# Paying out the convolution more densely beside two passes of matmuls, a new order of the second pass's first steps, and weights that load into space that is free earlier

## The chip, the cores and the metric

The kernel runs on one core of one Trainium2 chip. The metric is the device time in microseconds (us) from launch to end, as the median of several executions. Before the change it is 3131.01 us (three runs, 3129.59 to 3134.88). All data is float32.

The core has a matrix engine (PE, with a separate row PEld for its weight loads), a vector engine (DVE), a scalar engine (ACT), a GpSimd engine (POOL), and a queue (SP) that issues the transfers between DRAM, where all large tensors live, and the on-chip memory.

## What is computed

Two layers on an image batch of shape (2, 56, 56, 384). Layer 0 is neighbourhood attention (12 heads, 7 x 7 windows) followed by an MLP; layer 1 is a depthwise 3 x 3 convolution with four exponential scans, between two projections, followed by an MLP:

```python
# layer 0
h = neighborhood_attention(layer_norm(x), w_qkv, rpb, w_proj)
x = x + h
x = x + gelu(layer_norm(x) @ w1 + b1) @ w2 + b2              # 384 -> 1536 -> 384
# layer 1
p = layer_norm(x) @ w_in + b_in                              # 384 -> 768
local = depthwise_conv_3x3(p)                                # 768 channels
mixed = 0.25 * (scan_right(local) + scan_left(local)         # y[t] = 0.6 y[t-1] + 0.4 x[t]
                + scan_down(local) + scan_up(local)) + local
x = x + layer_norm(mixed) @ w_out + b_out                    # 768 -> 384
x = x + gelu(layer_norm(x) @ w1 + b1) @ w2 + b2
```

So three stages follow one another: attention; a *first pass* over tokens (MLP of layer 0, then the projection w_in of layer 1); and a *second pass* (projection w_out and MLP of layer 1). Between the two passes stands the convolution with its scans, which DVE computes channel block by channel block (6 blocks of 128 channels per image) while PE runs the passes.

## The kernel before

The passes run over groups of 512 tokens (4 tiles of 128). Group 0 of the first pass has only one tile. The order of instructions in the two passes is the order of the program text, on every engine. The convolution is cut into small steps, and a bookkeeper, `Beside`, hands them out between the matmuls:

```python
class Beside:
    def __init__(self):
        self.jobs, self.due, self.finished, self.idle = [], 0.0, set(), True
        self.late, self.rate = [], 0.85
    # ...
    def go(self, worth):                 # called after every few matmuls
        self.due += self.rate * worth    # pays out steps until the debt is gone
        while self.due > 0.0:
            step = self.step()           # emits one step, returns its size in us
            if step is None: self.due = 0.0
            else:            self.due -= step

    def until(self, name):               # emits steps until that job is done
        while name not in self.finished: self.step()
        # ...
MLP, PRO, ROW = 2.0, 2.5, 5.6            # first pass: per hidden block, per w_in block, per tile
MLP_D, OUT_D, ROW_D = 1.85, 2.2, 6.3     # second pass
```

A job is a `Band` (rows lo to hi of one channel block: one ACT copy, eight multiply-adds on DVE for the taps, two scans along the rows, one mixing operation) or, when all bands of an image are in, a `Columns` job (the scans along the columns: it loads the result of the bands back from DRAM, ACT turns it, DVE scans it and adds it to `mix_d`). Job `(1, 5)` is the last one: image 1, block 5.

```python
class Columns:
    def turn(self):                      # 4 ACT copies out of the loaded halves
        # ...
        nc.scalar.copy(t[...], self.loc[h][:, :, at].rearrange("p h w -> p w h"))
    def steps(self):
        if not self.lines:
            self.turn()
            yield 2.5
        # ... scans on DVE, then mixed += share * scanned, then the store
```

The pools for the passes are opened when attention's pools are closed, so they share its space. The loads of the first pass:

```python
wp = ctx.enter_context(tc.tile_pool(name="w", bufs=1))        # w1, w2, w_in, w_out ...
gp = ...; io = ...                                            # hidden blocks; x, xn, hT, xc, mx
# ...
xs = {0: load_group(x1f, groups[0], "xa")}
w1, w2, s2 = load_w(0)                                        # w1 in three pieces
nc.sync.dma_start(out=w_in, ...)
load_w2(w2, s2)                                               # w2 in three pieces
xs[1] = load_group(x1f, groups[1], "xa")
load_row(0, "b2_0"); load_row(1, "b_out")
nc.sync.dma_start(out=w_out, ...)
```

First pass, one group (`hidden` is three matmuls and a Gelu on ACT; `tokens` is twelve or six matmuls into one of two banks, which DVE empties):

```python
for g, (t0, n) in enumerate(groups):
    for m in range(NHID):                                     # 12
        hid.append(hidden(w1, m, hT, n, "L0_conv_b1"))
        if m == 3 and g < last: norm_next = norm_of(x_next)   # DVE statistics, close on POOL
        if m == 2 and waiting is not None: waiting = normalize_x2(*waiting)
        if m == 6 and g < last: xn_next = normalized(norm_next, x_next, n_next)   # ACT
        beside.go(MLP)
    if waiting is not None: project_in(*waiting)              # 6 blocks of w_in, beside.go(PRO)
    if g < last: hT = channels(xn_next, ...)                  # PE transposes, ACT evicts
    for k in range(n):
        ps = tokens(hid, w2, k)
        nc.vector.tensor_tensor(x2[:, k, :], ps, x[:, k, :], ALU.add)
        norm.add(k, [x2[:, k, :]])
        beside.go(ROW)
    waiting = g, x2, norm
```

Between the passes, and the second pass:

```python
w1, w2, s2 = load_w(1)
beside.until((0, NI - 1))
ahead = load_mix(0)                       # convolution's result of the first 512 tokens
project_in(*normalize_x2(*waiting))       # last group of the first pass
load_row(0, "b2_1"); load_w2(w2, s2)
for k in range(4): measure(ahead[0], ahead[2], k)     # PE transposes, DVE statistics
ahead[2].close(4)
x3, norm = project_out(0, *ahead)         # 4 tiles of w_out, beside.go(OUT_D)
ahead = load_mix(1)
xn = normalized(norm, x3, 4)
hT = channels(xn, ...)
for g, (t0, n) in enumerate(dgroups):
    for m in range(NHID):
        hid.append(hidden(w1, m, hT, n, "L1_conv_b1"))
        # measure() of group g + 1 beside m = 3, 5, 7, 9
        beside.go(MLP_D)
    if g < last: x3, norm = project_out(g + 1, *ahead)
    if g + 2 <= last and g + 2 != half_way: ahead = load_mix(g + 2)
    for k in range(n):
        ps = tokens(hid, w2, k)
        nc.vector.tensor_tensor(o, ps, o, ALU.add)            # o: the residual, then stored
        if k == 0 and g < last: xn = normalized(norm, x3, ...)
        beside.go(ROW_D)
    if g + 2 == half_way:                 # here g = 4: group 6 is the first with image 1
        beside.until((1, NI - 1))
        ahead = load_mix(g + 2)
    if g < last: hT = channels(xn, ...)
```

Of the kernel before, what the change touches and what calls it, by code (L numbers as in the profile page):

```python
# [30 lines left out]
F32 = mybir.dt.float32  # L31
# [8 lines left out]
P = 128  # L40
NC = C // P
# [47 lines left out]
class Beside:  # L89
# [2 lines left out]

    def __init__(self):
        self.jobs, self.due, self.finished, self.idle = [], 0.0, set(), True
        self.late, self.rate = [], 0.85
        self.steps = self.run()

    def behind(self, kind=object):
# [51 lines left out]
def block_kernel(ctx: ExitStack, tc: tile.TileContext, ins: dict, out: bass.AP):  # L150
# [81 lines left out]


    with ExitStack() as actx:
        wp = actx.enter_context(tc.tile_pool(name="a_w", bufs=1))
        io = actx.enter_context(tc.tile_pool(name="a_io", bufs=2))
        sm = actx.enter_context(tc.tile_pool(name="a_small", bufs=4))
        bp = actx.enter_context(tc.tile_pool(name="a_bias", bufs=2))
        at = actx.enter_context(tc.tile_pool(name="a_att", bufs=3))
# [12 lines left out]
            xg0[b, g] = t  # L252

        load_x(0, 0)
        wqkv = wp.tile([P, NC, 3 * C], F32, name="wqkv")
        nc.sync.dma_start(out=wqkv, in_=ins["L0_conv_w_qkv"].rearrange("(c p) n -> p c n", p=P))
        rows = wp.tile([TT, 2, C], F32, name="rows_a")
        for r in range(2):
            nc.sync.dma_start(out=rows[:, r, :], in_=ins["rows"][r : r + 1, :].to_broadcast([TT, C]))


        rpbt = wp.tile([TT, NH, UR, UC], F32, name="rpbt")
        for r in range(QR):
            nc.sync.dma_start(
                out=rpbt[r * QC : (r + 1) * QC],
# [254 lines left out]


    ctx.enter_context(tc.manual_schedule())
    wp = ctx.enter_context(tc.tile_pool(name="w", bufs=1))
    gp = ctx.enter_context(tc.tile_pool(name="g", bufs=NHID))
    io = ctx.enter_context(tc.tile_pool(name="io", bufs=2))
    sm = ctx.enter_context(tc.tile_pool(name="small", bufs=4))
    cp = ctx.enter_context(tc.tile_pool(name="conv", bufs=2))
    ps_m = ctx.enter_context(tc.tile_pool(name="psm", bufs=3, space=PSUM))
    ps_y = ctx.enter_context(tc.tile_pool(name="psy", bufs=2, space=PSUM))
    ps_t = ctx.enter_context(tc.tile_pool(name="pst", bufs=3, space=PSUM))  # L530


    groups = [(0, 1)] + [(t, NT) for t in range(P, T2, MT)]
# [12 lines left out]

    def load_group(src, group, tag):
        t0, n = group
        t = io.tile([P, NT, C], F32, name=tag)
        nc.sync.dma_start(  # L550
            out=t[:, :n, :], in_=src[t0 : t0 + n * P, :].rearrange("(k p) c -> p k c", p=P)
        )
        return t

    def load_w(layer):
        w1 = wp.tile([P, NC, HID], F32, name=f"w1_{layer}", tag="w1")
        w2 = wp.tile([P, NHID, C], F32, name=f"w2_{layer}", tag="w2")
        s1 = ins[f"L{layer}_conv_w1"].rearrange("(c p) n -> p c n", p=P)
        s2 = ins[f"L{layer}_conv_w2"].rearrange("(c p) n -> p c n", p=P)
        for h in range(0, HID, HID // 3):  # L560
            nc.sync.dma_start(out=w1[:, :, h : h + HID // 3], in_=s1[:, :, h : h + HID // 3])
        return w1, w2, s2
# [3 lines left out]
            nc.sync.dma_start(out=w2[:, c : c + NHID // 3, :], in_=s2[:, c : c + NHID // 3, :])  # L566

    x1f = x1_d.rearrange("b h w c -> (b h w) c")
    xs = {0: load_group(x1f, groups[0], "xa")}
    w1, w2, s2 = load_w(0)  # L570
    w_in = wp.tile([P, NC, INNER], F32, name="w_in")
    nc.sync.dma_start(out=w_in, in_=ins["L1_conv_w_in"].rearrange("(c p) n -> p c n", p=P))
    load_w2(w2, s2)
    xs[1] = load_group(x1f, groups[1], "xa")
    rows = wp.tile([P, 2, C], F32, name="rows")

    def load_row(i, name):
        r = ROWS[name]
        nc.sync.dma_start(out=rows[:, i, :], in_=ins["rows"][r : r + 1, :].to_broadcast([P, C]))

    load_row(0, "b2_0")
    load_row(1, "b_out")
    w_out = wp.tile([P, NI, C], F32, name="w_out")
    nc.sync.dma_start(out=w_out, in_=ins["L1_conv_w_out"].rearrange("(c p) n -> p c n", p=P))

    def row(name):
        return rows[:, 1 if name == "b_out" else 0, :]
# [1 line left out]
    def add_row(x, n, name):  # L589
# [2 lines left out]
        engine.tensor_tensor(  # L592
            x[:, :n, :], x[:, :n, :], row(name).unsqueeze(1).to_broadcast([P, n, C]), ALU.add
        )


    decay = wp.tile([P, LINES, W], F32, name="decay")
    nc.vector.memset(decay, DECAY)
    nc.vector.memset(decay[:, :, 0:1], 0.0)
    decay = decay.rearrange("p r w -> p (r w)")  # L600


    taps = wp.tile([P, 9 * NI], F32, name="taps")
    nc.vector.tensor_scalar_mul(
        taps, chan[:, COL["L1_conv_k_conv"] : COL["L1_conv_k_conv"] + 9 * NI], 1.0 + 0.5 * GAIN
    )

    def prepare_w_out():

# [28 lines left out]
            nc.vector.tensor_tensor(w_out[:, c, :], w_out[:, c, :], ps, ALU.subtract)  # L638

    def normalized(norm, x, n):  # L640
        xn = io.tile([P, NT, C], F32, name="xn")
        norm.apply_by_scalar(x, n, xn)
        return xn

# [188 lines left out]
                beside.later(store)  # L833


    MLP, PRO, ROW = 2.0, 2.5, 5.6
    MLP_D, OUT_D, ROW_D = 1.85, 2.2, 6.3

    def norm_of(x, n):
        norm = Norm(sm)  # L840
# [1 line left out]
            norm.add(k, [x[:, k, :]])  # L842
        return norm

    x = xs.pop(0)
    norm = norm_of(x, groups[0][1])
    norm.close(groups[0][1])
    xn = normalized(norm, x, groups[0][1])  # L850
    add_row(x, groups[0][1], "b2_0")
    hT = channels(xn, groups[0][1], "L0_conv_ln2_g", "L0_conv_ln2_b")
    waiting = None
    bands = [(b, lo, hi) for b in range(B) for lo, hi in BANDS[b]]

# [35 lines left out]
    for g, (t0, n) in enumerate(groups):  # L891
        hid = []
        preparing = prepare_w_out() if g == 1 else iter(())
        for m in range(NHID):
            next(preparing, None)
            hid.append(hidden(w1, m, hT, n, "L0_conv_b1"))
            if m == 3 and g < last:
                x_next, n_next = xs.pop(g + 1), groups[g + 1][1]
                norm_next = norm_of(x_next, n_next)
                norm_next.close(n_next)  # L900
            if m == (8 if g == 1 else 2) and waiting is not None:
                waiting = normalize_x2(*waiting)
            if m == 6 and g < last:
                xn_next = normalized(norm_next, x_next, n_next)
                add_row(x_next, n_next, "b2_0")
            beside.go(MLP)
        for _ in preparing:
            pass
        if waiting is not None:
            project_in(*waiting)  # L910
        if g < last:
            hT = channels(xn_next, n_next, "L0_conv_ln2_g", "L0_conv_ln2_b")
        x2 = io.tile([P, NT, C], F32, name="xc")
        norm = Norm(sm)
# [5 lines that stand above are left out]
        norm.close(n)  # L920
        waiting = g, x2, norm
        if g + 2 <= last:
            xs[g + 2] = load_group(x1f, groups[g + 2], "xa")
        if g < last:
            x = x_next

    def load_mix(g):
        t0, n = dgroups[g]  # L930
        mx = io.tile([P, NI, MT], F32, name="mx")
        for b, at, here, n in images(t0, n * P):
            nc.sync.dma_start(
                out=mx[:, :, here : here + n],
                in_=mix_d[b][:, :, at : at + n].rearrange("m p t -> p m t"),
            )
        x = load_group(x2_d, dgroups[g], "xa")
        if g >= half_way:
            add_row(x, dgroups[g][1], "b_out")
        return mx, x, Norm(sm)  # L940

    def measure(mx, norm, k):
        parts = []
        for h in range(2):
            ps = ps_t.tile([P, NC, P], F32, name="xi", tag="pt")
            for c in range(NC):
                nc.tensor.transpose(  # L947
                    ps[:, c, :], mx[:, h * NC + c, k * P : (k + 1) * P], ident
                )
            parts.append(ps.rearrange("p c q -> p (c q)"))  # L950
        norm.add(k, parts)

    def project_out(g, mx, x, inner):
        n = dgroups[g][1]
        x3 = io.tile([P, NT, C], F32, name="xc")
        norm = Norm(sm)
        for k in range(n):
            ps = tokens([mx[:, c, :] for c in range(NI)], w_out, k)
            nc.vector.scalar_tensor_tensor(
                x3[:, k, :], ps, inner.rs[:, k : k + 1], x[:, k, :], ALU.mult, ALU.add  # L960
            )
            norm.add(k, [x3[:, k, :]])
            beside.go(OUT_D)
        norm.close(n)
        return x3, norm

    w1, w2, s2 = load_w(1)
    beside.until((0, NI - 1))
    ahead = load_mix(0)
    project_in(*normalize_x2(*waiting))  # L970
    load_row(0, "b2_1")
    load_w2(w2, s2)
    for k in range(dgroups[0][1]):
        measure(ahead[0], ahead[2], k)
    ahead[2].close(dgroups[0][1])
    x3, norm = project_out(0, *ahead)
    ahead = load_mix(1)
    xn = normalized(norm, x3, dgroups[0][1])
    add_row(x3, dgroups[0][1], "b2_1")
    hT = channels(xn, dgroups[0][1], "L1_conv_n2_g", "L1_conv_n2_b")  # L980
    for g, (t0, n) in enumerate(dgroups):
        hid = []
        for m in range(NHID):
            hid.append(hidden(w1, m, hT, n, "L1_conv_b1"))
            if g < last and m % 2 == 1 and 0 <= m // 2 - 1 < dgroups[g + 1][1]:
                measure(ahead[0], ahead[2], m // 2 - 1)
            if g < last and m == 10:
                ahead[2].close(dgroups[g + 1][1])
            beside.go(MLP_D)
        res = x3  # L990
        if g < last:
# [79 lines left out]
```

## Time and profile before

| What | Value |
|---|---|
| Median of three runs | 3131.01 us |
| Profiled span | 3130.7 us |
| PE busy | 2930.5 us (94%) |
| DVE busy | 1664.2 us (53%) |
| ACT busy | 1065.2 us (34%) |
| DRAM traffic over the span | 87 GB/s |

Attention takes about the first 985 us, the first pass runs to about 2000 us, the second pass to the end; DVE has convolution work from about 1210 us to about 2555 us. The page's slices cut the span into 40 equal parts of 78 us, in which a digit is a tenth of busy time. The view of waits tells, for each line, how long an engine stood idle until a named instruction released it. The chain of waits follows the work that ended last back to the start; its columns are the start, the duration and what it was, with the number of instructions. In both, L numbers are lines of the kernel: L654 is the matmul of `hidden` and of the w_in projection, L670 the matmul of `tokens`, L226 and L229 the transposes and ACT evictions of `channels`, L215 the normalization on ACT, L947 the transposes of `measure`, L663 the Gelu, L795 the ACT copies of `Columns.turn`, L748 the taps of the convolution.

### The profile page before, as it was taken

The page shows a single profiled execution, that of the slowest core. Times are in us where ns is not written, and L with a number is a line of the kernel's source. Part 1 is how long each engine was busy: PE and PEld are TensorE (multiplying, and loading weights), DVE is VectorE, ACT ScalarE, POOL GpSimd, SP SyncE. Part 2 cuts the span into 40 slices and gives each one's busy share as a digit, 9 for nine tenths or more (in the row PEclk, how much of TensorE's full clock was granted, in tenths as well). Part 3 has the DMA queues.
Part 4 walks back from the last instruction along what each step waited for, and adds up shares of the span by engine and source line. Part 5 has one row for each costly group of instructions (what it writes and reads, how often), then busy time and mean ns, then how long its engine had stood idle before and what let it go on. Part 6 is the DMA issues. An engine that isn't in the chain of part 4 may idle for free.

```text
span 3130.7 us, 35981 instructions
## 1 busy us (share of the span) xinstructions
PE 2930.5 (94%) x13647; PEld 1609.2 (51%) x13647; DVE 1664.2 (53%) x3426; ACT 1065.2 (34%) x2506; POOL 337.0 (11%) x260
## 2 busy tenths in 40 slices
PE   6999999999996999999999999899998549999999
PEld 3555555555554555555555455445554325555555
DVE  3555555555454111777787787768886861111110
ACT  1555555555564222333332543121223221111111
POOL 2311022410021011000000000000000001111100
PEclk9999999999998999999999999999999869999999
DMA  6222222221124011222223543432324451111000
GB/s 140 72 61 61 64 60 73 65 63 56 55 65 141 18 41 55 98 104 103 100 91 122 197 169 144 167 141 101 120 85 150 154 184 41 40 41 41 18 10 13
DMA packets 130734, 275.87 MB, mean 88 GB/s; under 512 B 10192, under 2 KB 85440, under 8 KB 130560
## 3 DMA queue, kind: packets, MB, share of 16 engines
q1 hardware_dynamic: 130560, 273.57, 26.3%
q8 instruction: 107, 1.75, 0.2%
q14 instruction: 67, 0.55, 0.1%
HBM read 157.93 MB, written 115.61 MB: 87 GB/s over the span
## 4 chain that ended last, share of the span: by engine, by line
PE 79%; DVE 7%; DMA 6%; ACT 3%; issue 3%; POOL 2%; SPq 1%; POOLq 0%; ACTq 0%; DVEq 0%
PE y L670 29%; PE mm L654 27%; PE pt L422 4%; PE tp L294 4%; PE tp L466 3%; PE sc L392 3%; PE tp L315 3%; PE o L439 2%; DMA xg<-in_x 2%; PE tp L226 2%; DMA mixed<-mix_d 1%; DVE loc L748 1%; ACT pr L408 1%; DVE st L192 1%; PE xi L947 1%
## 5 line engine op out<-in xcount | busy, mean ns | idle before, releaser
L654 PE MATMUL mm<-hT,w 128*128 128x512 f32 (+1 forms) x1872 | 785.6, 576 | 88.1 <-ACT hT L229 69.7
L670 PE MATMUL y<-w,hid 128*128 128x384 f32 x2352 | 762.9, 486 | 0.0
L670 PEld LDWEIGHTS y<-w,hid 128*128 128x128 f32 x2352 | 446.1, 190 | 308.4 <-issue 0.5
L654 PEld LDWEIGHTS mm<-hT,w 128*128 128x128 f32 x1872 | 346.4, 194 | 479.3 <-issue 367.0
L663 ACT ACTIVATE hid<-mm,chan 128x512 f32<-128x512 f32 (+1 forms) x312 | 204.1, 660 | 723.1 <-PE mm L654 720.8
L408 ACT ACTIVATE pr<-pr,nm 112x238 f32<-112x238 f32 (+3 forms) x672 | 326.8, 488 | 226.9 <-DVE nm L401 223.9
L748 DVE SCALAR_TENSOR_TENSOR loc<-pt,taps,loc 128x990 f32<-128x990 f32 (+9 forms) x336 | 377.2, 1123 | 17.3 <-ACT loc L730 8.9
L401 DVE CUSTOM_DVE_ANT_0 pr<-sc,bias 112x238 f32<-112x238 f32 (+3 forms) x672 | 240.7, 407 | 170.4 <-PE sc L392 166.3
L200 POOL TENSOR_TENSOR rs<-rs,mhalf 128x4 f32<-128x4 f32 (+2 forms) x66 | 86.8, 1315 | 1836.3 <-DVE rs L197 1826.6
L294 PE MATMUL tp<-hT,wqkv 128*128 128x448 f32 x504 | 212.2, 554 | 7.9 <-DVE qT L300 4.9
L422 PE MATMUL pt<-ident,pr 112*100 112x112 f32 (+5 forms) x1584 | 209.3, 271 | 9.8 <-ACT pts L427 9.8
L422 PEld LDWEIGHTS pt<-ident,pr 112*100 112x100 f32 (+5 forms) x1584 | 162.9, 148 | 81.0 <-issue 53.3
L654 PE MATMUL mm<-hT,w_in 128*128 128x512 f32 (+1 forms) x468 | 194.7, 575 | 4.4 <-ACT hT L229 3.6
L670 PE MATMUL y<-w_out,mx 128*128 128x384 f32 x588 | 191.8, 486 | 0.0
L229 ACT ACTIVATE hT<-tp,chan 128x512 f32<-128x512 f32 (+2 forms) x159 | 109.0, 743 | 237.7 <-PE tp L226 233.5
L215 ACT ACTIVATE xn<-xc,sh,rs 128x384 f32<-128x384 f32 x98 | 61.4, 696 | 319.4 <-DVE sh L211 319.3
L917 DVE TENSOR_TENSOR xc<-y,xa 128x384 f32<-128x384 f32 x49 | 27.3, 558 | 253.8 <-PE y L670 253.7
L392 PE MATMUL sc<-kT,qT 32*112 32x238 f32 (+3 forms) x1344 | 157.4, 416 | 0.0
L670 PEld LDWEIGHTS y<-w_out,mx 128*128 128x128 f32 x588 | 111.6, 190 | 80.2 <-issue 5.7
L192 DVE BATCH_NORM_STATS2 st<-xi 128x6 f32<-128x384 f32 x98 | 50.3, 554 | 189.7 <-PE xi L947 189.6
L998 DVE TENSOR_TENSOR xc<-y,xc 128x384 f32<-128x384 f32 x49 | 27.2, 555 | 231.2 <-PE y L670 188.2
L427 ACT COPY pts<-pt 80x448 f32<-80x448 f32 (+3 forms) x228 | 117.4, 515 | 85.9 <-PE pt L422 85.9
(74 smaller groups left out, 2766.8 us busy)
## 6 DMA issues: line engine op xcount, KB each, us to landing
loc<-loc_d SPq DMA_DIRECT2D x24, 784.0 KB
mixed<-mix_d SPq DMA_DIRECT2D x24, 784.0 KB
mix_d<-mixed SPq DMA_DIRECT2D x24, 784.0 KB
xa<-x_d SPq DMA_DIRECT2D x24, 768.0 KB
p_d<-mx SPq DMA_DIRECT2D x11, 1536.0 KB
mx<-mix_d SPq DMA_DIRECT2D x11, 1536.0 KB
pt<-p_d SPq DMA_DIRECT2D x18, 560.0 KB
xg<-in_x SPq DMA_DIRECT2D x14, 672.0 KB
```

The costliest lines, as they stand in the source:

```text
L229: nc.scalar.activation(dst[:, c, : len(xs) * n], tp, AF.Identity, bias=col(b, c), scale=col(g, c))
L294: nc.tensor.matmul(ps, lhsT=wqkv[:, c, m * P : (m + 1) * P], rhs=hT[:, c, :], start=c == 0, stop=c == NC - 1,)
L315: nc.tensor.matmul(ps, lhsT=hT[:, c, k * TT : (k + 1) * TT], rhs=wqkv[:, c, 2 * C :], start=c == 0, stop=c == NC - 1,)
L392: nc.tensor.matmul(ps[:, : w.nk], lhsT=qTs[w.b, w.g][d, hg, w.j, :], rhs=kT[d, hg, w.r0 : w.r0 + w.kr, w.c0 : w.c0 + w.kc], start=True, st ...
L401: nc.vector.tensor_tensor_reduce(out=self.pr[:, i, : w.nk], in0=ps[:, : w.nk], in1=w.bias[:, 4 * hg + i, : w.nk], scale=-1.0, scalar=BIG, ...
L408: nc.scalar.activation(self.pr[:, i, : w.nk], self.pr[:, i, : w.nk], AF.Exp, bias=nm[:, i : i + 1], scale=-1.0, accum_out=w.sums[:, h : h ...
L422: nc.tensor.transpose(tp[:n, i, :], self.pr[:, i, a : a + n], idt)
L427: nc.scalar.copy(t[:n], tp[:n])
L654: nc.tensor.matmul(ps[:, : n * P], lhsT=w[:, c, m * P : (m + 1) * P], rhs=hT[:, c, : n * P], start=c == 0, stop=c == NC - 1,)
L663: nc.scalar.activation(t[:, : n * P], ps[:, : n * P], AF.Gelu, bias=col(b1, m))
L670: nc.tensor.matmul(ps, lhsT=t[:, k * P : (k + 1) * P], rhs=w[:, m, :], start=m == 0, stop=m == len(lhs) - 1,)
L748: nc.vector.scalar_tensor_tensor(to, pt[:, lo + dy - self.top : hi + dy - self.top, xt : xt + n], self.tap(dy, dx), to, ALU.mult, ALU.add,)
```

## The change

There are four parts.

1. The convolution is paid out more densely: the rate for image 0 and all payments but PRO go up, so that the convolution of each image is done earlier.
2. The order between the passes is another. The first mixed group is loaded at the start of the first pass's last group and measured beside its hidden blocks; `project_out(0)` follows at once on the last tiles; only then comes the `project_in` of the last group.
3. The pools of the passes are split: `w_mlp` (w1, w2) and `x` (xa, xn) are opened first and lie where attention's `a_first` (w_qkv and the bias table) and `a_io` lie, which attention is done with before its end. The loads of w1, w2 and of the first two groups come first; w_in, w_out and the row vectors come later.
4. The PSUM pool of the hidden blocks is opened last of the three.

The diff, cut (`[...]` marks cuts; code that only moves is named):

```diff
-        self.late, self.rate = [], 0.85
+        self.late, self.rate = [], 0.9
 [...] attention
+        fp = actx.enter_context(tc.tile_pool(name="a_first", bufs=1))
+        io = actx.enter_context(tc.tile_pool(name="a_io", bufs=2))
         wp = actx.enter_context(tc.tile_pool(name="a_w", bufs=1))
-        io = actx.enter_context(tc.tile_pool(name="a_io", bufs=2))
-        wqkv = wp.tile([P, NC, 3 * C], F32, name="wqkv")
+        wqkv = fp.tile([P, NC, 3 * C], F32, name="wqkv")
-        rpbt = wp.tile([TT, NH, UR, UC], F32, name="rpbt")
+        rpbt = fp.tile([TT, NH, UR, UC], F32, name="rpbt")
 [...] the passes
+    wm = ctx.enter_context(tc.tile_pool(name="w_mlp", bufs=1))
+    xp = ctx.enter_context(tc.tile_pool(name="x", bufs=2))
     wp = ctx.enter_context(tc.tile_pool(name="w", bufs=1))
-    ps_m = [...] "psm", bufs=3      (moved behind ps_y and ps_t)
-    xs = {0: load_group(x1f, groups[0], "xa")}
     w1, w2, s2 = load_w(0)
+    xs = {g: load_group(x1f, groups[g], "xa") for g in range(2)}
+    load_w2(w2, s2)
-    nc.sync.dma_start(out=w_in, ...); load_w2(w2, s2); xs[1] = ...
-    load_row(0, "b2_0"); load_row(1, "b_out"); nc.sync.dma_start(out=w_out, ...)
 [...]
-    MLP, PRO, ROW = 2.0, 2.5, 5.6
-    MLP_D, OUT_D, ROW_D = 1.85, 2.2, 6.3
+    MLP, PRO, ROW = 2.25, 2.5, 6.2
+    MLP_D, OUT_D, ROW_D = 2.15, 2.5, 7.0
 [...] after channels() of group 0
+    load_row(0, "b2_0"); load w_in; load w_out; load_row(1, "b_out")
+    (the memsets of decay and the taps stand here now)
 [...] in the loop of the first pass
+        if g == last:
+            beside.until((0, NI - 1))
+            load_row(0, "b2_1")
+            ahead = load_mix(0)
+            if g == last:                       # in the loop over m
+                measure_beside(m, 0, ahead)
+        if g == last:                           # after project_in(group last - 1)
+            w1, w2_1, s2 = load_w(1)
 [...] between the passes
-    w1, w2, s2 = load_w(1); beside.until((0, NI - 1)); ahead = load_mix(0)
-    project_in(*normalize_x2(*waiting))
-    load_row(0, "b2_1"); load_w2(w2, s2)
-    for k in range(4): measure(...)
-    ahead[2].close(4)
+    waiting = normalize_x2(*waiting)
     x3, norm = project_out(0, *ahead)
-    ahead = load_mix(1)
     xn = normalized(norm, x3, dgroups[0][1])
     add_row(x3, dgroups[0][1], "b2_1")
+    ahead = load_mix(1)
+    w2 = w2_1
+    load_w2(w2, s2)
+    project_in(*waiting)
     hT = channels(xn, dgroups[0][1], "L1_conv_n2_g", "L1_conv_n2_b")
```

## The prediction

> **What bounds the kernel now.** I read the page first, then the view of PE's waits, then the chain of waits in order of time, and last the sums of single stages.
>
> ```profile
> PE 2930.5 (94%) x13647; PEld 1609.2 (51%) x13647; DVE 1664.2 (53%) x3426; ACT 1065.2 (34%) x2506; POOL 337.0 (11%) x260
> ...
> PE   6999999999996999999999999899998549999999
> ...
> DVE  3555555555454111777787787768886861111110
> ...
> PEclk9999999999998999999999999999999869999999
> ```
>
> PE is the bound, and no matmul is removed, so only its holes can be won. There are three: the start of the first pass (13th slice, a 6), a shallow one before slice 30, and a deep one in slices 32 and 33 (5 and 4), where the clock also falls to 8 and 6 tenths. DVE stands at 6 to 8 tenths ahead of the deep hole and at 1 tenth behind it.
>
> ```profile
> PE mm L654 <- ACT hT L229: 73.3, 9, 61.2
> PE tp L226 <- ACT xn L215: 23.4, 3, 9.2
> PE mm L654 <- ACT hid L663: 18.3, 5, 14.0
> ...
> PE xi L947 <- DMA mx<-mix_d: 14.8, 1, 14.8
> ```
>
> All of PE's idle time is 196.6 us (the gaps between its busy spans, added up). Single waits carry most: 61.2 and 14.8 us in the deep hole, 8.2 us before it, 9.2 and 14.0 us at the start of the first pass, 8.1 and 6.1 us between the passes. Attention's waits (62.8 us together before 980 us, in the same view) are untouched.
>
> ```profile
> 2251.38 46.44 PE y L670 x144
> ...
> 2332.93 23.23 PE y L670 x72
> ...
> 2374.82 7.49 DMA loc<-loc_d
> 2383.15 4.98 ACT line L795 x6
> ...
> 2424.78 23.23 PE y L670 x72
> ...
> 2482.54 3.31 DMA mix_d<-mixed
> 2485.87 8.23 DMA mixed<-mix_d
> ...
> 2551.10 3.35 DMA mix_d<-mixed
> 2554.51 7.55 DMA mx<-mix_d
> ...
> 2588.10 46.44 PE y L670 x144
> 2669.64 46.44 PE y L670 x144
> ```
>
> The y rows mark the group of the second pass. An undisturbed group takes 2669.64 - 2588.10 = 81.54 us, also 2332.93 - 2251.38 = 81.55. The group after 2332.93 takes 91.85 us (10.3 lost), the next 163.32 us (81.8 lost). In the last one the chain leaves PE and runs through `mixed` and `mix_d`: that is `until((1, 5))`, which empties the rest of the convolution with nothing beside it. The 10.3 are another cause: the first `Columns` job of image 1 waits for its load, ACT stands in `turn` (L795), and hT waits behind it on ACT.
>
> [...] between 2052 and 2460 us a scan of 18 or 20 lines took 2.36 us, a tap of the same bands 1.29 us.
>
> ```profile
> L748 DVE SCALAR_TENSOR_TENSOR loc<-pt,taps,loc 128x990 f32<-128x990 f32 (+3 forms) x98 | 126.6, 1292 | 4.4 <-ACT loc L730 2.3
> L695 DVE TENSOR_TENSOR_SCAN both<-decay,loc 128x1008 f32<-128x1008 f32 (+1 forms) x13 | 30.7, 2361 | 0.3
> ```
>
> [...] a clock of 0.72 from 2500 to 2600 us, with PE busy 51%. So a hole costs a few us more than its length. [...]
>
> **Part 1, the payments.** I add up the bookkeeper's own numbers. Per group of the second pass it pays 12 x 1.85 + 4 x 2.2 + 4 x 6.3 = 56.2 before and 12 x 2.15 + 4 x 2.5 + 4 x 7.0 = 63.8 after. Five groups, one `project_out` and one `project_in` lie before the wait: 5 x 56.2 + 8.8 + 15 = 305 before, 5 x 63.8 + 10 + 15 = 344 after. A group of the first pass pays (12 x 2.0 + 6 x 2.5 + 4 x 5.6) x 0.85 = 52.2 before and 66.8 x 0.9 = 60.1 after; from image 1 on (rate 1) 61.4 and 66.8. Following the program text step by step, 538.5 units are done before the second stretch, of 922.5 in all: 844.4 at the wait, 78.1 left. After, it comes out at none left, the last step about 11 us of matmuls ahead of the wait. A unit is 0.93 us on DVE: all convolution lines together are 857.9 us for 922.5 units. So 78.1 units are 73 us of DVE, plus the waits for DRAM between the jobs: this is the 81.8. The mixed load (7.55 us in the chain) then has the hT transposes and four hidden blocks (about 10 us) to land in.
>
> The 10.3 us: after, the first `Columns` of image 1 begins in the middle of `project_out`, some 35 us of matmuls ahead of the next hT. The turn then holds no hT back, but DVE waits for it (8.1 us in the trace), and y has two banks of 3.87 us each there. I leave 5 us of the 10.3. Part 1 saves 81.8 + 10.3 - 5 = 87.
>
> **What part 1 costs.** From 2052 to 2460 us (five groups) DVE was busy 314.8 us, of which 74.5 are not convolution: 14.9 per group. A band's steps run at 0.965 us per unit (1.29 for a tap booked at 1.25 to 1.37, 2.36 for a scan at 2.4 to 2.7), so a group after needs 63.8 x 0.965 + 14.9 = 76.5 of 81.5 us: 94%, against 69.1 (85%) before. In `project_out` it is 2.5 x 0.965 + 1.41 = 3.8 of 3.87 us per tile, in the last tiles about 31 of 31 us: just full, with a reserve only in the hidden blocks. PE feels DVE through y's two banks. I put 1 us per group: 5. In the first pass the statistics at m = 3 (4 x 0.73 = 2.9 us) and three payments lie before the normalization at m = 6 (3 x 2.62 = 7.9 us of matmuls): 3 x 1.64 + 2.9 = 7.8 before and 3 x 1.95 + 2.9 = 8.8 after for image 0, 8.7 and 9.4 for image 1. Where this is over 7.9, ACT waits with the Gelus behind it; such waits were at most 1.5 us (4 times, 4.3 us in all between 1070 and 1990 us). I put 6 us more over eleven groups.
>
> **Part 3, the loads.** Before, PE stood 9.2 us (982.2 to 991.4), then ran ten hidden blocks of group 0, stood 14.0 us until 1015.55 because the first xa of group 1 came behind w1, w_in and w2, and ended the twelve at 1018.5. After, in the order on the queue, all of w1, w2 and both xa stand before the last windows of attention. The 14.0 go. Of the 9.2 only about 2 go: the statistics still wait for attention's last stores, which free the small tiles; before, xa itself landed at 988.5. Saved: 16. The loads are 5.6 MB over attention's last 45 us; before, x, w1, w_in and w2 (6.6 MB, in 22 us) moved at some 300 GB/s, so they take 19 us. A window's vt load has some 13 us from issue to use (944 to 957.5 us), so I expect no new wait.
>
> **Part 2, the order.** Before, from the last tile (1995.6) to the first y of the second pass (2088.3) passed 92.7 us. The matmuls need 17.2 (project_in with its transposes) + 3.3 (measure) + 15.5 (project_out) + 1.7 (transposes) + 34.3 (hidden blocks and measure) = 72.0; so 20.7 are lost, with 14.2 as the two waits for xn and the rest as slow clock and filling. After, `project_out(0)` starts at once: the first wait goes. [...] last statistics (1.4), a payment (2.4), POOL (1.5), four ACT instructions (2.5) and hT (0.75), with 1.5 us of transposes against it. So a hole of about 7 us comes back there, and I count half of the 20.7: 10. The memory of part 4 touches no path.
>
> **The sum.** 3131 - 87 + 5 + 6 - 16 - 10 = 3029; with the clock regained where small holes vanish (2 us), 3027.
>
> **The rivals.** (a) DVE becomes the bound. At 94% on average and 100% in the last tiles each late tap would hold y, and the holes would be spread instead of gone. For it: payments of 3.8 in 3.87 us, and waits of DVE itself for `mixed` (8.3 us in 7 waits, 2052 to 2570 us) which come on top. Against it: before, from 2052 to 2330 us, PE had no wait at all at 85%, and the hidden blocks leave 4 us per group. It would give back 20 to 40 us: 3050 to 3070. (b) The wait at `until` is replaced by the one for the mixed load, because the last stores are late: before, PE stood 14.8 us for it. Against it are the 11 us of lead; it would cost 10: 3037. (c) The loads of w1 and w2 hold back attention's vt and xr: 5 to 10 us. (d) All density is free and the Columns wait goes wholly: 3010.
>
> **Range and chances.** (d) is the low end and a mild (a) with (b) the high end: 3008 to 3056 holds it 8 times in 10. Faster by over 2% means under 3068; only a full (a) together with (c) reaches that: 0.93. Within 2%: 0.06. Slower: 0.01; the removed 76 us of waits would have to be paid back twice.
>
> **What would show it.** The profile after should have no PE wait over 10 us after attention, the y rows about 82 us apart up to the half-way group, DVE at 8 to 9 tenths from 1300 to 2450 us and PEclk at 9 in slices 32 and 33. At the start: no wait of hid for ACT of 14 us, but about 7 us for xn. Between the passes: one wait of about 7 us for hT. I am wrong if waits for DVE at y or for hT behind ACT add up to over 25 us, if the mixed load still waits at the half-way group, or if attention ends later than 982 us.

## The result, and the profile after the change

The changed kernel takes 3060.12 us (median of 4 runs, 3058.47 to 3061.64); the kernel before, run beside it on the same chip, took 3132.28. The ratio is 0.977, with a 95% interval of 0.9753 to 0.9787. The change saves 72 us. The prediction said 104 and a range up to 3056, so the time lies 4 us outside it.

The page of the changed kernel, with the shares of busy time and the slices (tenths, 40 slices):

```profile
PE 2932.8 (96%) x13647; PEld 1607.4 (53%) x13647; DVE 1661.1 (54%) x3426; ACT 1063.1 (35%) x2506; POOL 336.9 (11%) x260
...
PE   6999999999998899999999999989999999999999
...
DVE  3555555555555211585788788978998841111110
...
PEclk9999999999999999999999999999999999999999
```

The deep hole of slices 32 and 33 is gone, with its slow clock: 0.72 was granted from 2500 to 2600 us before, 1.00 from 2515 to 2600 us now. It had cost 81.8 us, 5.8 more than its two waits of 61.2 and 14.8. PE's busy time is what it was (2930.5), so the 72 us are holes: PE's idle time fell from 196.6 to 122.1 us. The 13th slice, a 6 before, is an 8. PE's waits, all of the kernel (us in total, times, longest):

```profile
...
PE mm L640 <- ACT hid L649: 20.0, 10, 4.6
...
PE tp L226 <- ACT xn L215: 11.6, 1, 11.6
PE mm L640 <- ACT hT L229: 9.7, 6, 7.3
...
...
PE xi L849 <- DMA mx<-mix_d: 3.5, 1, 3.5
PE y L656 <- DVE xc L869: 3.2, 1, 3.2
```

The wait of 61.2 us for hT is gone, and so is the one of 14.0 us for `hid` at the start. But behind attention `hid` is still the largest: 20.0 us, now in ten waits of at most 4.6, of which nine (18.9 us) lie inside the first pass. Before, that stretch had four such waits of 4.3 us together. The chain of waits, with the groups marked by their y rows (start, us). First the kernel before:

```profile
1073.97 30.96 PE y L670 x96
...
1964.64 23.23 PE y L670 x72
...
2088.30 46.44 PE y L670 x144
```

then the changed kernel:

```profile
1072.78 30.96 PE y L656 x96
1153.17 30.96 PE y L656 x96
...
1318.69 30.98 PE y L656 x96
...
1404.87 30.98 PE y L656 x96
...
1492.61 30.98 PE y L656 x96
...
1988.42 30.98 PE y L656 x96
...
2101.06 23.23 PE y L656 x72
...
2427.71 23.23 PE y L656 x72
...
2481.75 7.61 DMA mx<-mix_d
...
2515.79 46.44 PE y L656 x144
```

In the second pass the four groups from 2101.06 to 2427.71 take 326.65 us, 81.7 each, and the half-way group 88.08. In the first pass a group takes 80.39 us (1153.17 - 1072.78) as long as nothing is paid out beside it, but 86.2 (1318.69 to 1404.87) and 87.7 (to 1492.61) with it. Subtracting the starts of the y rows in the two chains gives the whole account:

| Stretch | before, us | after, us | difference | predicted |
|---|---|---|---|---|
| start to the first full group's y | 1073.97 | 1072.78 | -1.2 | -16 |
| from there to the last group's y, first pass | 890.67 | 915.64 | +21.6 (*) | +6 |
| from there to the first y of the second pass | 123.66 | 112.64 | -7.6 (*) | -10 |
| from there to the half-way group's y | 499.80 | 414.73 | -85.1 | -82 |
| the rest, to the end of the span | 542.6 | 542.7 | 0 | 0 |

(*) The 24 transposes of `measure` (0.14 us each, 3.4 us) moved from the third stretch into the second; the two differences are +25.0 and -11.0 with them. The 2 us that the prediction added for the clock were an estimate and belong to no single row.

So two rows are as predicted, and two are off by about 15 us each. The experiments ask why the first pass got slower, and where the gain at the start went.

### The profile page after: what moved, and what is told of

Its sections match the earlier page's. It is cut to its first block, busy times and chain, and to the rows that moved or that the text cites. A ratio compares the mean times of both kernels' runs of the same rounds, so it can differ in the third digit from the quotient of the medians.

```text
span 3058.5 us, 35962 instructions
## 1 busy us (share of the span) xinstructions
PE 2932.8 (96%) x13647; PEld 1607.4 (53%) x13647; DVE 1661.1 (54%) x3426; ACT 1063.1 (35%) x2506; POOL 336.9 (11%) x260
## 4 chain that ended last, share of the span: by engine, by line
PE 78%; DVE 10%; DMA 5%; ACT 3%; issue 2%; POOL 1%; SPq 0%; ACTq 0%; POOLq 0%; DVEq 0%
PE y L656 29%; PE mm L640 24%; PE tp L296 5%; PE pt L424 5%; PE tp L468 4%; DVE loc L734 4%; PE sc L394 3%; PE tp L317 3%; PE o L441 2%; DMA xg<-in_x 2%; PE tp L226 1%; DVE st L192 1%; ACT xn L215 1%; DMA x_d<-xr 1%; PE xi L849 1%
## 5 line engine op out<-in xcount | busy, mean ns | idle before, releaser
L468 PE MATMUL tp<-wproj,oT 128*112 128x384 f32 x336 | 131.8, 532 | 23.5 <-DVE qT L302 22.6
L1009 DVE TENSOR_TENSOR xc<-y,xc 128x384 f32<-128x384 f32 x49 | 27.1, 554 | 227.7 <-PE y L656 184.6
```

The source lines that it names most:

```text
L468: nc.tensor.matmul(ps, lhsT=w.oT[:, c, :], rhs=wproj[:, c, :], start=c == 0, stop=c == NC - 1)
```

## The experiments

### The first pass: what holds the Gelu back

The group with the longest wait of `hid` shows it. Timeline of the changed kernel (start, length, engine, line, operation; idle time before it and what ended that). The group begins at 1435.67 us with m = 0:

```profile
1435.67 25.91 PE L640 MATMUL mm<-hT,w 128*128 128x512 f32 x60
...
1449.54 1.76 DVE L590 TENSOR_TENSOR xc<-xc,rows 128x1536 f32<-128x1536 f32 x1 [2.57 <-ACT xn L215]
...
1452.37 0.55 DVE L192 BATCH_NORM_STATS2 st<-xa 128x6 f32<-128x384 f32 x1
...
1455.24 5.12 DVE L734 SCALAR_TENSOR_TENSOR loc<-pt,taps,loc 128x990 f32<-128x990 f32 x4
...
1455.49 1.86 POOL L200 TENSOR_TENSOR rs<-rs,mhalf 128x4 f32<-128x4 f32 x1 [11.48 <-DVE rs L197]
...
1460.39 2.26 DVE L681 TENSOR_TENSOR_SCAN both<-decay,loc 128x1008 f32<-128x1008 f32 x1
...
1462.80 0.15 DVE L211 SCALAR_TENSOR_TENSOR sh<-mv,rs 128x4 f32<-128x4 f32 x1
1463.04 2.50 ACT L215 ACTIVATE xn<-xa,sh,rs 128x384 f32<-128x384 f32 x4 [8.39 <-DVE sh L211]
...
1466.16 2.07 PE L640 MATMUL mm<-hT,w 128*128 128x512 f32 x2 [4.58 <-ACT hid L649]
```

POOL has the reciprocal deviation `rs` ready at 1457.35 us. The next step, `sh` (minus mean times `rs`, 0.15 us), is a DVE instruction, and in program order it stands behind the payments of m = 3 to 5: four taps and a whole scan. It runs at 1462.80, 5.4 us late. ACT cannot start the normalization before, the next Gelus stand behind that on ACT, and PE, which has three banks for `mm`, stops for 4.58 us. Both queues ran in program order here: `sh` started 0.11 us after the last step ahead of it did, the normalization 0.24 us after `sh`, and the next Gelu behind the normalization at 1465.44. The same group in the kernel before:

```profile
1429.01 25.91 PE L654 MATMUL mm<-hT,w 128*128 128x512 f32 x60
...
1444.42 0.56 DVE L192 BATCH_NORM_STATS2 st<-xa 128x6 f32<-128x384 f32 x1
...
1452.33 0.15 DVE L211 SCALAR_TENSOR_TENSOR sh<-mv,rs 128x4 f32<-128x4 f32 x1
...
1455.65 4.56 PE L654 MATMUL mm<-hT,w 128*128 128x512 f32 x10 [0.73 <-ACT hid L663]
```

In both PE runs ten blocks (25.91 us) by itself and goes on 3.3 to 3.4 us after `sh`. So `sh` costs nothing up to some 22.6 us after the group's start. Before, it ran at 23.3 us, and PE stood 0.73; now it runs at 27.1, and PE stands 4.58.

The first theory was therefore: not the amount of DVE work is too much, but an instruction of 0.15 us that others wait for stands in its queue. The rival was the prediction's rival (a): DVE is simply too full.

**e1** takes that instruction out of DVE's queue behind the steps: DVE forms minus mean right beside the input of `rs`, and POOL multiplies.

```diff
 # Norm.close
+    nc.vector.scalar_tensor_tensor(self.sh[:n, :k], self.mv[:n, :k, 0], -1.0, ones[:n, :k], ALU.mult, ALU.mult)
     nc.gpsimd.tensor_tensor(rs, rs, mhalf[:n, :k], ALU.pow)
+    nc.gpsimd.tensor_tensor(sh, sh, rs, ALU.mult)
 # Norm.apply_by_scalar
-    nc.vector.scalar_tensor_tensor(sh[:, :n], self.mv[:, :n, 0], -1.0, self.rs[:, :n], ALU.mult, ALU.mult)
```

> The changed kernel, with the small product that gives ACT its bias (minus mean times rs, DVE L211) computed on POOL right behind rs instead of on DVE just ahead of the normalization. Theory A: in the first pass this instruction stands in DVE's queue behind the steps paid out since m = 3, and the Gelus stand behind the normalization on ACT. Then PE's waits of the hidden blocks for hid fall from 20.0 us in 10 waits to under 6 us, and the time falls by about 14 us to 3046. Rival B: DVE is simply full there, so that the statistics themselves and with them rs come late; or ACT is held by its copies for the convolution. Then hid waits stay above 15 us and the time is 3060 within 4 us.

It measured 3029.28 us (3027.04 to 3031.87), ratio 0.9675 (0.9661 to 0.969): 31 us faster than the changed kernel, twice what was expected. The same place in its timeline:

```profile
1442.99 5.12 DVE L739 SCALAR_TENSOR_TENSOR loc<-pt,taps,loc 128x990 f32<-128x990 f32 x4
...
1443.22 1.88 POOL L205 TENSOR_TENSOR rs<-rs,mhalf 128x4 f32<-128x4 f32 x1 [8.65 <-DVE rs L202]
...
1445.18 0.40 POOL L208 TENSOR_TENSOR sh<-sh,rs 128x4 f32<-128x4 f32 x1
...
1445.61 2.50 ACT L220 ACTIVATE xn<-xa,sh,rs 128x384 f32<-128x384 f32 x4 [0.77 <-POOL sh L208]
```

The normalization starts while the same four taps still run, and PE has no gap. Inside the first pass (1070 to 2000 us) 3.4 us in one wait of `hid` are left (ACT's copies for the first `Columns` job, whose load comes late), and the stretch from first to last group's y is 890.74 us instead of 915.64. The sums by stage (window, length; busy us and count of PE, PEld, DVE, ACT, POOL; granted clock, DMA share, GB/s) say the same. First the kernel before:

```profile
1240.00:1580.00 340.00, 335.47 (x955) 172.89 (x954) 249.84 (x267) 97.73 (x142) 17.33 (x8) 1.00 0.28 99
```

then the changed kernel, with its second pass in the second row:

```profile
1240.00:1580.00 340.00, 326.11 (x907) 165.64 (x906) 252.95 (x267) 97.75 (x143) 17.36 (x8) 0.98 0.28 99
2101.00:2428.00 327.00, 326.75 (x1011) 179.24 (x1010) 286.08 (x319) 93.56 (x125) 12.63 (x9) 1.00 0.44 156
```

and e1:

```profile
1240.00:1580.00 340.00, 339.44 (x970) 176.35 (x969) 267.48 (x290) 99.56 (x144) 21.85 (x16) 1.00 0.29 104
```

In e1 DVE does more in the window than in either of the others (267.48 us of 340), and PE stands for half a microsecond. A too full DVE would have stopped PE more. The rival falls for the first pass; the row of the second pass refutes it there too. The saving was mis-sized because only PE's waits had been counted: the clock of the window rose from 0.98 to 1.00 with them (0.02 x 340 = 7 us in this window alone); over the whole first pass the same 792 matmuls of hidden blocks keep PE busy 343.0 us before, 352.5 in the changed kernel and 344.6 in e1. And the half-way group of the second pass went from 88.1 to 84.0 us. Of the latter the wait for the mixed load explains 1.3 us (3.5 to 2.2); the rest was not traced.

**e8** leaves `sh` where it is and pays out unevenly, with the same sum per group: little after m = 2 to 5, more elsewhere.

```diff
-            beside.go(MLP)
+            beside.go(0.75 if 2 <= m <= 5 else 3.0)
```

> The changed kernel with the same payments per group of the first pass in another split: 0.75 after the hidden blocks m = 2 to 5 and 3.0 after the other eight, instead of 2.25 after each of the twelve. Theory: only the steps that stand in DVE's queue between the statistics (m = 3) and the normalization (m = 6) hold ACT up. Then PE's waits for hid between 1070 and 2000 us fall from 18.9 us to under 6, the first pass gets 15 to 22 us shorter, and the time is 3040, though DVE has the same work. Rival: it is the density as such, which DVE can't work off in a group; then the waits stay, or move to y and to hT: 3058 to 3062.

3040.75 us (3037.37 to 3045.34), ratio 0.9717 (0.9701 to 0.9733), 19 us faster than the changed kernel. PE's waits between 1070 and 2000 us in it:

```profile
PE mm L640 <- ACT hid L649: 6.6, 6, 1.8
```

The work and its density over the group are the same; what stands ahead of `sh` decides.

**e6** is the kernel before with the new payments alone (part 1).

```diff
-        self.late, self.rate = [], 0.85
+        self.late, self.rate = [], 0.9
-    MLP, PRO, ROW = 2.0, 2.5, 5.6
-    MLP_D, OUT_D, ROW_D = 1.85, 2.2, 6.3
+    MLP, PRO, ROW = 2.25, 2.5, 6.2
+    MLP_D, OUT_D, ROW_D = 2.15, 2.5, 7.0
```

> The kernel before with the eight numbers of the payments alone. Theory: it takes 76 us of waits and some clock from the half-way group and the 10 us before it (85 us from the first y of the second pass to the half-way group), and gives 22 us back in the first pass to PE's waits for hid: 3068. If the rest of the change were needed for the gain, or if the first pass's loss came from the new pools or the new order of loads, the first pass would stay within 3 us of before and the time would be 3047.

3078.2 us (3073.93 to 3081.59), ratio 0.9828 (0.9811 to 0.9844). Its waits in the first pass:

```profile
PE mm L654 <- ACT hid L663: 19.9, 9, 4.6
```

By the y rows of its chain the second pass up to the half-way group takes 413.04 us (86.8 less than before) and the first pass 914.67 us (24.0 more). So the payments alone bring the whole gain of the second pass and the whole loss of the first; the new order and the loads have no part in either. Between the passes it takes 128.44 us, 4.8 more than before, with a wait of 11.2 us for xn there: the old order costs more beside dense payments. Against that the new order is worth 15.8 us (128.44 to 112.64), 12.4 without the moved `measure`. The time of e6 is 10 us over the expected 3068: besides the 4.8 us between the passes, the first pass lost 2 more than reckoned, and its first full group began 3.0 us later than before.

### Between the passes: hT behind another normalization

The prediction's returning hole is there: 7.28 us, where about 7 were worked out. Timeline of the changed kernel:

```profile
2045.43 2.50 ACT L215 ACTIVATE xn<-xc,sh,rs 128x384 f32<-128x384 f32 x4 [12.11 <-DVE sh L211]
2047.84 2.09 ACT L229 ACTIVATE hT<-tp,chan 128x512 f32<-128x512 f32 x3
...
2048.65 13.73 PE L640 MATMUL mm<-hT,w_in 128*128 128x512 f32 x28 [7.28 <-ACT hT L229]
```

The copies of hT need only transposes that end at about 2041.4, but stand on ACT behind the normalization of x3. **e3** puts them ahead of it.

```diff
     x3, norm = project_out(0, *ahead)
+    hT_in = channels(waiting[1], groups[last][1], "L1_conv_n1_g", "L1_conv_n1_b")
     xn = normalized(norm, x3, dgroups[0][1])
...
-    project_in(*waiting)
+    project_in(*waiting, hT_in)
```

> The changed kernel with the transposes and the ACT evictions of hT for the last project_in put ahead of the normalization of x3 in the program. Theory A: the 7.3 us of PE's wait for hT between the passes are ACT's order alone. Then this wait is under 1 us, the waits of x3's own hT stay hidden behind the six blocks of w_in, and the time falls by 8 to 10 us with the clock, to 3051. Rival B: the wait only moves, since the normalization of x3 then comes late for its own hT: 3058 to 3060.

3050.65 us (3050.21 to 3058.25), ratio 0.9749 (0.9734 to 0.9764): 9.5 us less. The wait of 7.3 us is gone from the list of waits and nothing came in its place; only the 3.2 us of y for xc are left there.

### The start: where the 14 us of the loads went

Attention ends at 982.2 us before and at 994.9 after. From its end to the first y of group 0 it takes 38.6 us before and 24.8 after. So the new order of loads does win 13.8 us behind attention, and attention itself loses 12.7. **e4** undoes parts 3 and 4 (pools and loads as before) and keeps the payments and the order of the second pass.

```diff
-    w1, w2, s2 = load_w(0)
-    xs = {g: load_group(x1f, groups[g], "xa") for g in range(2)}
-    load_w2(w2, s2)
+    xs = {0: load_group(x1f, groups[0], "xa")}
+    w1, w2, s2 = load_w(0)
+    # w_in, then w2, then xs[1], the rows and w_out; pools shared as before
```

> The changed kernel with the pools of the passes, the PSUM order and the loads of the first pass put back as before the change (payments and the order between the passes stay). Theory A: the new loads are worth almost nothing, since they remove 13 us of wait in group 0 but make attention's tail 6 us and the first statistics 2.4 us later: 3065. Theory of the prediction: they are worth 16 us: 3076. In both the wait of 14 us for hid at the start comes back.

3063.03 us (3061.2 to 3071.91), ratio 0.9788 (0.9767 to 0.981). The wait for `hid` is back, with 13.2 us, and yet the time is only 3 us longer (5.6 by the two ratios to the kernel before): parts 3 and 4 are worth 3 to 6 us, not 16. From the 52nd to the last of attention's 56 projections e4 takes 35.9 us (before: 34.2), the changed kernel 40.4. **c0** is the kernel before once more, to see how much attention varies by itself.

> The kernel before, once more, as a control: its attention is the same program as that of the changed kernel up to the last four windows, yet the changed kernel's 48th projection began 6.6 us later. If this is the spread of executions, the 48th projection begins anywhere from 897 to 904 us here and the tail behind it takes 83 us again; if the changed kernel slows attention, it begins at 897 us once more.

One run, 3135.65 us. Its 48th projection starts at 899.9 us, 2.7 later than in the first trace of the same kernel (897.2); from there to the 52nd it takes 51.9 us against 48.6, and from the 52nd to the last 34.2 in both. So the tail of 83 us that was expected became 86, and attention ended at 988.1 us, 5.9 later than in the first trace. Among four kernels with the new loads and the same text of attention the 48th starts between 895.4 and 903.8 us; in e4, with the old loads, at 903.1. So of the 12.7 us 6.2 are the last four projections and belong to the change; the other 6.6 lie ahead of them and are within what kernels with the old loads vary by too.

What happens in these last projections shows in the timeline (SPq is the queue that issues transfers). Before the change, a store and the load that follows it into the same buffer:

```profile
939.34 0.70 SPq L470 DMA_DIRECT2D x_d<-xr  x1
942.25 0.70 SPq L372 DMA_DIRECT2D xr<-in_x  x1
```

In the changed kernel:

```profile
946.20 0.94 SPq L565 DMA_DIRECT2D w<-in_L_conv_w  x2
947.25 0.70 SPq L472 DMA_DIRECT2D x_d<-xr  x1
...
953.84 0.72 SPq L374 DMA_DIRECT2D xr<-in_x  x1
...
958.38 0.99 POOL L375 TENSOR_TENSOR xr<-xr,rows_a 112x384 f32<-112x384 f32 x1 [11.76 <-DMA xr<-in_x]
959.31 0.50 POOL L454 COPY wide<-rec 112x384 f32<-112x384 f32 x1
```

The store of one window's result is issued at 947.25 us, behind two 768 KB pieces of w1. The load of a later window into the same buffer can go only when the store is done, and is issued at 953.84, 6.6 us later instead of 2.9. It lands at about 958.4, where POOL, first in its queue, waits to add the bias to it. Behind that addition stands the copy `wide`, which PE needs for another window: PE stood 2.9 us. The rest of the gain goes after attention:

```profile
995.43 0.42 SPq L885 DMA_DIRECT2D w_in<-in_L_conv_w_in  x1
995.90 0.65 SPq L472 DMA_DIRECT2D x_d<-xr  x1
...
1003.62 0.56 DVE L192 BATCH_NORM_STATS2 st<-xa 128x6 f32<-128x384 f32 x1 [8.10 <-DMA w_in<-in_L_conv_w_in]
```

Attention's last store is issued behind w_in, and the first pass's statistics start 7.7 us later. PE's wait for xn is 11.6 us, where 7 were predicted.

**e2** gives `xr` a fourth buffer (taking the room from two small pools) and issues rows, w_in and w_out from ACT's queue.

```diff
-                self.xr = at.tile([TT, C], F32, name="xr", bufs=3)
+                self.xr = at.tile([TT, C], F32, name="xr", bufs=4)
-    nc.sync.dma_start(out=w_in, in_=...)
+    nc.scalar.dma_start(out=w_in, in_=...)      # w_out and rows likewise
```

> The changed kernel with a fourth buffer for attention's residual rows xr, so that each is loaded one window earlier, and with the loads of w_in, w_out and the two row vectors issued from ACT behind the hT of group 0 instead of from SP ahead of attention's last store. Theory A: attention's last windows are 6 us late because xr waits behind the pieces of w1 and w2 in the same queue, and the first statistics are 2.4 us later than before because the last store stands behind w_in. Then the last projection of attention comes 6 us earlier against its 48th window, PE's wait for xn at the start falls from 11.6 to about 7.5 us, and the time is 3050. Rival B: [...] the tail stays 6 us late, only the 4 us at the start are won, and the time is 3056.

3058.93 us (3057.05 to 3060.24), no different from the changed kernel; 3050 or 3056 were expected. The wait for xn fell from 11.6 to 6.5 us, as it should with the store no longer behind w_in. The last four projections still took 42.3 us: with four buffers the scheduler moved the load and POOL's addition one window earlier too, and `wide` stood as before (3.4 us). This run doesn't tell whether POOL or the transfers hold attention back.

**e5** issues w1 and w2 from ACT's queue as well, so that no window's transfer stands behind them.

```diff
-    w1, w2, s2 = load_w(0)
+    w1, w2, s2 = load_w(0, nc.scalar)
-    load_w2(w2, s2)
+    load_w2(w2, s2, nc.scalar)
```

> The changed kernel with the six pieces of w1 and w2 issued from ACT instead of SP, and w_in, w_out and the row vectors from ACT behind the hT of group 0. Theory A: attention's tail is late because its last store, and with it the next xr, stands behind 1.5 MB of w1 in SP's queue. From the 48th to the last projection the changed kernel took 88.9 us (82.8 before); it should take 83 to 85 us here, and the time should be 3050. Rival B: [...] the tail stays at 88 to 89 us and the time is 3056, as with the late loads from ACT alone. A third way: ACT stands at the issues itself, and the tail gets longer than 89 us.

3053.93 us (3051.61 to 3059.43), ratio 0.9753 (0.9739 to 0.9768). The last four projections take 36.9 us and PE's waits for `wide` at the end of attention fall from 3.9 to 1.0 us. But from the 48th to the 52nd it takes 54.5 us, against 47.0 to 51.7 in the kernels that issue the early loads from SP, and a wait of PE for ACT's copy `pts` grows to 2.7 us. In sum 91.4 us, where theory A had 83 to 85: it wins at one place and loses at another. Whether ACT's issues are the cause (the third way) isn't shown: in that stretch ACT issues two pieces, 0.4 us each. The longest wait of SP's queue for a store of `xr` is 8.0 us here, 7.9 in the changed kernel and 2.2 before. So issuing the weights from another engine didn't make the store faster, and why the last four projections are shorter stays open.

### Together

**e7** is e1, e3 and e5 in one kernel.

> The changed kernel with all four repairs: the ACT bias from POOL, all weights of the first pass issued from ACT, and the hT of the last project_in ahead of x3's normalization. If they are independent, the sum is 3060 - 31 - 9.5 - 4 (late loads) = 3016, and 3011 if the queue also frees attention's tail. If the gain of the bias on POOL was partly luck of the clock, 3025.

3014.29 us (3009.15 to 3020.3), ratio 0.9625 (0.9609 to 0.9641), between the two sums of 3011 and 3016.

**e9** is e1, e3 and the loads of rows, w_in and w_out from ACT, with w1 and w2 left on SP; and POOL adds the bias behind the sum, where nothing waits for it, instead of ahead:

```diff
 # Window.__init__
-    nc.gpsimd.tensor_tensor(self.xr, self.xr, rows[:, ROWS["b_proj"], :], ALU.add)
 # project()
     nc.vector.tensor_tensor(w.xr, ps, w.xr, ALU.add)
+    nc.gpsimd.tensor_tensor(w.xr, w.xr, rows[:, ROWS["b_proj"], :], ALU.add)
```

> The changed kernel with the ACT bias from POOL, the hT of the last project_in first, w_in, w_out and the row vectors from ACT behind group 0's hT, w1 and w2 from SP as in the change; and in attention POOL adds b_proj behind the sum instead of ahead of it, so that its copy of the denominators no longer stands behind the load of xr. Theory: this wait of POOL is the 6.6 us that the loads cost between the 52nd and the last projection (41.3 us in the kernels with the new loads, 34.8 with the old). It should be 35 to 37 us here, and the time 3010. Rival: the late store and vt hold attention up by themselves: 41 us again, and 3016.

3007.03 us (2999.2 to 3012.03), ratio 0.9606 (0.9589 to 0.9624): 53 us faster than the changed kernel and the fastest of all. POOL in its timeline, in the same part of attention:

```profile
951.06 0.50 POOL L458 COPY wide<-rec 112x384 f32<-112x384 f32 x1 [6.19 <-PE pt L428]
...
953.60 1.00 POOL L476 TENSOR_TENSOR xr<-xr,rows_a 112x384 f32<-112x384 f32 x1 [2.03 <-DVE xr L475]
```

Now `wide` comes first, and no transfer ends its wait; the addition follows it and waits for the sum. The waits for `wide` are gone, the last four projections take 35.2 us with w1 and w2 in SP's queue as in the changed kernel, and attention ends at 978.5 us. Its other edits alone left those projections slow (e1 41.8, e3 40.8, the late loads in e2 42.3 us), so it is POOL's place in the chain that cost most of the 6 us: SP's queue still waits up to 8.0 us for a store of `xr`, but nothing urgent waits behind the load that follows.

## Why the prediction was wrong, point by point

- **The gain of part 1 in the second pass: right.** 85.1 us against 82 (81.8 + 10.3 - 5 - 5). The stretch of steps with nothing beside it is gone; 3.5 us of PE's wait for the mixed load are left, rival (b) in small and one of the prediction's signs of being wrong. The two deductions of 5 us were too high: the four full groups cost 326.65 - 4 x 81.54 = 0.5 us more than undisturbed ones, and the `Columns` group none. What was left is the half-way group: 88.08 - 81.54 = 6.5.
- **The cost of part 1 in the first pass: the step that failed.** The prediction compared 3 x 1.95 + 2.9 = 8.8 us of DVE work (7.8 before the change) with 7.9 us of matmuls and wrote "I put 6 us more over eleven groups". It was 21.6. The place was right: the normalization, with the Gelus behind it. What failed is where the sum starts and what reserve it gives. It lets DVE begin the statistics when PE begins m = 3, 7.7 us after the group's start. In the first four groups with payments DVE began them 15.8 to 17.7 us after it (14.5 to 15.7 before): ahead of them stand the payments of the last tile and of m = 0 to 2, and with x2's normalization a wait of 2.0 to 2.6 us until ACT has read x2 and the addition of `b_out` to it (1.4 to 1.8 us). From the statistics to `sh` it took 8.9 to 10.4 us, close to the 8.8. So `sh` ran 25.1 to 27.1 us after the start, against 22.6 to 23.6 before: on average 2.7 us later, 1.5 of them ahead of the statistics, where the sum did not look, and 1.2 behind them, where it had 1.0. And there was no reserve: before the change `sh` already stood at or just over the limit of 22.6, so nearly every added us became a wait of PE. e1 and e8 show that the queue ahead of `sh` is the cause of these waits, e6 that the payments alone bring them about. Eight of the nine waits (15.4 us) are this, five at the normalization of m = 6 and three at that of x2 (m = 2). The ninth, 3.45 us at 1712.6 us, is ACT's wait for the load of the first `Columns` job, and it stays in e1. The waits of `hid` and hT together grew by 13.1 us (20.7 against 7.6); the rest is a slower clock (0.99 was granted from 1070 to 1990 us, 1.00 before): the same matmuls of the hidden blocks take 9.5 us more (352.5 against 343.0).
- **The start: the second term that failed.** 1.2 us against 16. The 14.0 us of `hid` went, as said. Rival (c), "the loads hold back attention's vt and xr: 5 to 10 us", was right with 6.2, and was put aside because vt had 13 us to spare; "attention ends later than 982 us" was a sign of being wrong that came true. But the tight path was not vt: it was a store, the load that reuses its buffer, and POOL. Behind attention, the wait for xn got longer instead of shorter (9.2 to 11.6, not 7), because the last store stood behind w_in; e2 shows that (6.5). The other 6.6 us by which attention ended later lie within its variation (e4, with the old loads, was as late there); a part due to the change can't be excluded from these runs.
- **Between the passes: right.** 7.6 against 10, and the hole of 7.28 us for hT where 7 was worked out. e3 shows the cause, the order on ACT: with the copies of hT first, the wait is gone. The granted clock between the passes was 0.91 before (1995 to 2089 us) and 0.95 after (1990 to 2101 us).
- **Rival (a), DVE as the bound: wrong.** 286.08 of 327 us busy, 87%, and PE stands 0.3 us in all. The prediction's 94% put a group at 76.5 us of DVE work; 286.08 / 4 = 71.5 were measured. Its own trace could have warned it: the 314.8 us of five groups are 63.0 each, where its formula gives 69.1.

## What to carry to other kernels

Filler work beside matmuls was cheap here even with DVE 87% busy (PE stood 0.3 us in 327), as long as no small instruction that others wait for stood behind it in the same queue: follow each chain of engines through to its last link, and move a link to an idle engine or thin out the filler just ahead of it. Measure from where that chain really starts, and how much reserve it has left: here it had none. Early loads of large weights delayed the small stores beside them here (from the issue of a store to that of the next load into its buffer, 2.9 us became 6.6; with the weights issued from ACT the longest wait for such a store was 8.0 us, 7.9 without); look for the buffer whose store they delay, and for the engine that waits first for its next load, as POOL did here for 11.76 us with `wide` behind it.

## What the runs showed of the hardware

- Small POOL operations took longer beside DVE's taps and scans. In the kernel before, the power of 128 x 4 numbers took 1.02 us at 1011.49 us, ahead of the convolution, and 3.00 at 1272.54 us, beside a scan of 2.38 us. In e1 the multiplication of 128 x 4 numbers took 0.20 us wherever DVE was idle and up to 2.24 elsewhere, the power of the same size 1.01 us with DVE idle and up to 3.00; all that took over 1.1 us lay beside a tap, a scan or a mixing operation of DVE. The longest, from 2005.60 us on, ends with the scan of 2.22 us beside it. On DVE the product takes 0.14 to 0.17. So the move to POOL cost 0.25 us at 1445.18, where it won 5.4 of queue, and up to 2.1 elsewhere.
- Two executions of the kernel before ended attention at 982.2 and 988.1 us, and in kernels that differ only behind it its 48th projection began between 895.4 and 903.8 us. A gain of a few us in a single trace's attention says little.
